# Between two edge passes of a graph network: another order for the first five tiles, and ScalarE's order written out

## The chip, the cores and the metric

The kernel runs on one core of a Trainium2 chip. The metric is device time in microseconds (us), the median of several executions. A core has five engines that run beside each other, each through its own queue in order: PE (TensorE, matrix products and transposes), DVE (VectorE), ACT (ScalarE), POOL (GpSimd, here the issuer of gathers) and SP (SyncE, here the issuer of DMA transfers).

## The reference

Two layers of a graph network on 3125 nodes with 256 features and 103125 edges. Each layer adds a graph part and an attention-like part to x, and then a mixture of experts. Cut to what lies around the change:

```python
xn = _layernorm(x)
x = x + edge_max(xn, src, dst) + mix0(xn)            # first edge pass
z = _layernorm(x)
x = x + layer_norm(moe(z) + z) * gamma + beta        # two experts for all tokens
xn = _layernorm(x)
# second edge pass: relational graph convolution
W = einsum("rb,bio->rio", comp, basis)               # 8 relations
h_all = einsum("ni,rio->nro", xn, W)                 # a table of 3125 x 8 rows
agg = segment_sum(h_all[src, edge_type], dst)
x = x + layer_norm(gelu(agg + xn @ loop_w + h_bias + xn)) + attention(xn)
x = x + moe(layer_norm(x))                           # top 2 of 8 experts for each token
```

Layer 0's router works on the mean over all nodes, so both experts and their weights are the same for all tokens, but known for certain only once every node has gone through the first pass.

## The kernel before, in words

The nodes lie in 25 tiles of 128 (the last is short). In the first pass POOL gathers rows of neighbours, DVE takes the maximum, and a queue of background jobs works off what follows. The experts are guessed from the means of the first tiles and their products run in the background of the pass. At its end tile 0 alone is left: `settle` fixes the router's weights (`w_first`, the first expert's weight, L1491) and whether the guess failed (`missed`, L1489); PE has meanwhile computed tile 0's hidden products into two PSUM banks (`phs`, `hidden_products`, L1515). All engines then read `missed` (L1953) and branch (L1954); the body of that branch, which repeats the experts' work with other weights, is not entered in these runs.

The stretch after the branch makes the second pass's table, tile by tile from tile 24 down to tile 0. A class `Four` takes the tiles in groups of `cuts`: two (24, 23), three (22 to 20), four, four, four, four, three and one. A group's vector work has four steps, each a list of one job for each tile:

- `mixed` (L2008): z is the sum of both experts' outputs, with statistics; after the last tile ScalarE takes a square root (L2016).
- `added` (L2020): subtract the mean, scale.
- `summed`: reciprocal (L2025), add to x (L2026), statistics; after the last tile a second root (L2032).
- `normed`: reciprocal (L2037), normalize (L171); z is then ready for its table.

`table(j, between)` makes the table of one tile: `to_xT` transposes z on PE (L182) and copies it on ScalarE (L183); four blocks of products follow (L188, 512 columns each; `mm`, four PSUM banks), each evacuated into `hs` by ScalarE (blocks 0 and 2, L177) or DVE (blocks 1 and 3, L175; for tile 24 all four on DVE, L2057); then SP stores 1 MB to `htab` (L2061). After each block the jobs of `between[b]` are issued: the steps of the next group, and after them sums of early gathers (L2114). How they are spread is this line, for the list `mine` of a table's jobs:

```python
per = -(-len(mine) // 4)
four.table(j, [mine[per * b : per * (b + 1)] for b in range(4)])
```

`early` lets POOL fetch own rows and, from about the tenth table on, edge rows of four tiles whose tables are ready. Which, and when, is fixed when the program is built.

Inside `tc.manual_schedule(engines=...)` the named engines run in the program's order; the other engines' order is chosen by the framework's planner. Before, DVE and POOL are named, so ScalarE and PE are planned: ScalarE may copy the transposed z of two tiles ahead of evacuations and roots. Tile 0's gelus (`hidden_gelus`, L1524), output products (`outputs_a`: two bias matmuls L1529, sixteen matmuls L1532) and their copies (`outputs_out`, L1542 and L1543) come in the program ahead of the first table; `outputs_b` follows five tables later.

In this text tables and joins are counted from 0: table 0 is tile 24's, table 24 is tile 0's, and join 5-6 is the place between tables 5 and 6. After the tables the second pass gathers with POOL, and its background jobs hold attention and the experts.

Of the kernel before, what the change touches and what calls it, by code (L numbers as in the profile page):

```python
# [11 lines left out]
F32 = mybir.dt.float32  # L12
BF16 = mybir.dt.bfloat16
I32 = mybir.dt.int32
AF = mybir.ActivationFunctionType
# [5 lines left out]
P = 128  # L21
# [33 lines left out]
GROUPS = tuple(range(a, b) for a, b in zip(CUTS, CUTS[1:])) + (range(0, 1),)  # L55
# [45 lines left out]
def gps_kernel(ctx: ExitStack, tc: tile.TileContext, a, out):  # L101
    nc = tc.nc
    V, S, G, PE = nc.vector, nc.scalar, nc.gpsimd, nc.tensor
# [45 lines left out]
    def bcast_load(name, ap, n, pool):  # L149
        t = pool.tile([P, n], F32, name=name)  # L150
        S.dma_start(t, bass.AP(tensor=ap.tensor, offset=ap.offset, ap=[[0, P], [1, n]]))
        return t
# [801 lines left out]
    with ExitStack() as prx:  # L954
        prx.enter_context(
            tc.manual_schedule(
                engines={mybir.EngineType.DVE, mybir.EngineType.Pool, mybir.EngineType.PE, mybir.EngineType.SP}
# [328 lines left out]
        steps = pre.tile([P, NT], F32, name="steps")  # L1286
# [31 lines left out]
    def fast():  # L1318
# [76 lines left out]
        mv2 = keep.tile([P, NT, 2], F32, name="mv")  # L1395
        rs2 = keep.tile([P, NT], F32, name="rs")
        f0k = f0h = f0b = None
        w1 = w2 = b1 = b2 = w_rel = basis = gam = bet = w_first = missed = guessed = part = inside = None
        pmean = [None]

        def begin():
            nonlocal f0k, f0h, f0b, w1, w2, b1, b2, w_rel, basis, gam, bet, w_first, missed, guessed, part, inside
            f0k = f0x.enter_context(tc.tile_pool(name="f0k", bufs=1, side="right"))
            f0h = f0x.enter_context(tc.tile_pool(name="f0h", bufs=2, side="right"))
            f0b = f0bx.enter_context(tc.tile_pool(name="f0b", bufs=1, side="right"))
            w1 = f0k.tile([P, 2, 2, F], F32, name="w1_0")
            w2 = f0k.tile([P, 2, FC, D], F32, name="w2_0")
            b1 = f0k.tile([P, 2, FC], F32, name="b1_0")
            b2 = f0k.tile([1, 2, D], F32, name="b2_0")
            w_rel = f0k.tile([P, 2, NX * D], F32, name="w_rel")  # L1410
            w_first = f0k.tile([P, 1], F32, name="w_first")
            missed = f0k.tile([1, 1], I32, name="missed")
            guessed = f0k.tile([P, 2, NX], F32, name="guessed")
            part = f0k.tile([P, 2], F32, name="part")
            basis = f0b.tile([P, 4, 2, D], F32, name="basis")
            for b in range(4):
                nc.sync.dma_start(basis[:, b, :, :], a["basis"][b].rearrange("(c p) o -> p c o", p=P))
            gam = bcast_load("gam0", a["f0_gamma"], D, f0k)
            bet = bcast_load("bet0", a["f0_beta"], D, f0k)
            inside = f0k.tile([P, 1], F32, name="inside")  # L1420
            V.tensor_scalar(inside, pcol, LAST - 0.5, None, op0=ALU.is_lt)
# [56 lines left out]
        def settle():  # L1478

            mean = f0k.tile([P, 2], F32, name="mean_b")  # L1480
            V.tensor_tensor(mean, part, pmean[0], op=ALU.add)
            V.tensor_scalar(mean, mean, 1.0 / NN, None, op0=ALU.mult)
            w_full, rank = settled[:] = yield from route(mean, "b")
            tmp = f0k.tile([P, NX], F32, name="tmp_b")
            hit = f0k.tile([P, 2], F32, name="hit")
            V.tensor_tensor(tmp, guessed[:, 0, :], guessed[:, 1, :], op=ALU.add)
            V.scalar_tensor_tensor(tmp, rank[:, 0, :], 1.5, tmp, op0=ALU.is_lt, op1=ALU.mult)
            V.reduce_sum(hit[:, 0:1], tmp, axis=AX.X)
            V.tensor_scalar(missed, hit[0:1, 0:1], 1.5, None, op0=ALU.is_lt)  # L1489
            V.tensor_tensor(tmp, w_full[:, 0, :], guessed[:, 0, :], op=ALU.mult)  # L1490
            V.reduce_sum(w_first, tmp, axis=AX.X)  # L1491
# [17 lines left out]
        def hidden_products(ts, i, ph=None):  # L1509

            at0 = ts[0] * P
            ph = ps_mm.tile([P, 512], F32, name="mm") if ph is None else ph
            for f in range(FC):
                for c in range(2):
                    PE.matmul(  # L1515
                        ph[:, f * P : (f + 1) * P], w1[:, i, c, f * P : (f + 1) * P], xT[:, c, at0 : at0 + P],
                        start=(c == 0), stop=(c == 1),
                    )
            return ph

        def hidden_gelus(ts, i, ph):
            hT = hTs[i] = f0h.tile([P, FC, 3 * P], F32, name=f"hT0_{i}", bufs=1)
            for f in range(FC):
                S.activation(hT[:, f, :P], ph[:, f * P : (f + 1) * P], AF.Gelu, bias=b1[:, i, f : f + 1])  # L1524

        def outputs_a(ts):
            for j, t in enumerate(ts):
                py = pys[t] = ps_mm.tile([P, 512], F32, name="mm")
                PE.matmul(py, ones_row, b2.rearrange("o i d -> o (i d)"), start=True, stop=True)  # L1529
                for i in range(2):  # L1530
                    for f in range(FC):
                        PE.matmul(  # L1532
                            py[:, i * D : (i + 1) * D], hTs[i][:, f, j * P : (j + 1) * P], w2[:, i, f, :],
                            start=False, stop=(f == FC - 1), skip_group_check=True,
                        )

        def outputs_out(ts):

            for t in ts:
                py = pys.pop(t)  # L1540
                y1 = seconds[t] = f0h.tile([P, D], F32, name="y1", bufs=SECONDS)
                S.copy(xT[:, :, t * P : (t + 1) * P], py[:, :D].rearrange("p (c n) -> p c n", c=2))  # L1542
                S.copy(y1, py[:, D:])  # L1543

        def outputs_b(ts):


            for t in ts:
                y1 = seconds.pop(t)
                d = xT[:, :, t * P : (t + 1) * P]  # L1550
                V.tensor_tensor(xt_tok[:, t, :], xt_tok[:, t, :], y1, op=ALU.add)
                V.tensor_tensor(d, d, y1.rearrange("p (c n) -> p c n", c=2), op=ALU.subtract)
# [12 lines left out]
        with ExitStack() as l0x:  # L1565
# [376 lines left out]
            ET = mybir.EngineType  # L1942
            with tc.manual_schedule(engines={ET.DVE, ET.Pool, ET.PE, ET.Activation}):
                fin[0].sums(0)
                fin[0].norms()
                routing = settle()
                next(routing)
                ts = GROUPS[-1]
                phs = [hidden_products(ts, i) for i in range(2)]
                for _ in routing:  # L1950
                    pass

        again = nc.values_load(missed[0:1, 0:1])  # L1953
        with tc.If(again > 0):  # L1954
# [33 lines left out]
        sump = fx.enter_context(tc.tile_pool(name="sump", bufs=1))  # L1988
        sums = sump.tile([P, len(EARLY), D], F32, name="sums")
        with ExitStack() as tx:  # L1990
            tx.enter_context(tc.manual_schedule(engines={mybir.EngineType.DVE, mybir.EngineType.Pool}))
            tp = tx.enter_context(tc.tile_pool(name="tp", bufs=2, side="right"))
            ready = []

# [130 lines left out]
            fours = [Four(range(a, b)) for a, b in cuts]  # L2125

            first, second = fours[0].steps(), fours[1].steps()
            for part_ in (first[0], second[0], first[1], second[1], first[2], first[3], second[2]):
                for job in part_:
                    job()  # L2130
            for i in range(2):
                hidden_gelus(GROUPS[-1], i, phs[i])
            outputs_a(GROUPS[-1])
            outputs_out(GROUPS[-1])
            for four, after in zip(fours, fours[1:] + [None]):
                steps = after.steps() if after is not None else []
                if four is fours[0]:
                    steps = second[3:]
                each = -(-len(steps) // four.k)
                if four is fours[2]:  # L2140
                    outputs_b(GROUPS[-1])
                for j in range(four.k):
                    mine = [job for part_ in steps[each * j : each * (j + 1)] for job in part_]
                    while adds and adds[0][0] + 4.0 < TABLE * len(ready):
                        mine.append(lambda a=adds.popleft(): add_up(*a[1:]))
                    per = -(-len(mine) // 4)
                    four.table(j, [mine[per * b : per * (b + 1)] for b in range(4)])
                    ready.append(four.tiles[j])
                    early(len(ready) - 1)
# [9 lines left out]
        with ExitStack() as l1x:  # L2159
# [18 lines left out]
            b1 = l1w.tile([P, NX, FC], F32, name="b1")  # L2178
# [401 lines left out]
    with tc.If(unfit < 1):  # L2580
        fast()
# [78 lines left out]
```

## Time and profile before

| | |
|---|---|
| median of 6 runs | 2987.46 us (2967.22 to 2996.63) |
| the profiled execution | 2989.64 us |
| its span | 2987.9 us |
| granted TensorE clock, mean | 0.762 |
| busy: PE, PE weight loads, DVE, ACT, POOL | 63%, 40%, 42%, 19%, 58% |
| end of the first pass's routing (w_first) | 1428.2 us |
| first table product | 1445.16 us |
| last store of the table issued | 1643.2 us |
| second pass's own gathers begin | 1660.49 us |

In a line of the profile's timeline stand the start (us from the span's start), the length, the engine, the line of the kernel, the operation, what it writes and reads with its size, and in square brackets how long the engine was idle before it and what ended that. Lines named PE are matmuls, PEld weight loads; a `q` behind an engine's name is its instruction queue.

### The profile page before, as it was taken

The page shows a single profiled execution, that of the slowest core. Times are in us where ns is not written, and L with a number is a line of the kernel's source. Part 1 is how long each engine was busy: PE and PEld are TensorE (multiplying, and loading weights), DVE is VectorE, ACT ScalarE, POOL GpSimd, SP SyncE. Part 2 cuts the span into 40 slices and gives each one's busy share as a digit, 9 for nine tenths or more (in the row PEclk, how much of TensorE's full clock was granted, in tenths as well). Part 3 has the DMA queues.
Part 4 walks back from the last instruction along what each step waited for, and adds up shares of the span by engine and source line. Part 5 has one row for each costly group of instructions (what it writes and reads, how often), then busy time and mean ns, then how long its engine had stood idle before and what let it go on. Part 6 is the DMA issues. An engine that isn't in the chain of part 4 may idle for free.

```text
span 2987.9 us, 20996 instructions
## 1 busy us (share of the span) xinstructions
PE 1881.3 (63%) x6033; PEld 1182.6 (40%) x6033; DVE 1256.7 (42%) x3537; ACT 558.5 (19%) x1275; POOL 1724.5 (58%) x1830
## 2 busy tenths in 40 slices
PE   4374657403473653366898348867786786866877
PEld 2232324202341422244443124554454454654656
DVE  7443434526324433344664333334343334343342
ACT  5122221000110101011321112122111121222233
POOL 5566566676647566655036755565666566656561
PEclk9675777655785776677899667887898888877978
DMA  5533333333323233322256632232232222222220
GB/s 178 137 86 91 82 87 101 93 107 110 93 62 105 67 96 85 94 67 77 97 197 223 197 111 67 80 89 80 84 92 86 78 82 82 86 77 84 76 80 18
DMA packets 125962, 290.09 MB, mean 97 GB/s; under 512 B 41386, under 2 KB 63982, under 8 KB 122632
## 3 DMA queue, kind: packets, MB, share of 16 engines
q0 software_dynamic: 83184, 230.02, 27.1%
q1 hardware_dynamic: 38122, 55.88, 5.5%
q10 hardware_dynamic: 4526, 2.71, 0.4%
q8 instruction: 51, 0.84, 0.1%
q14 instruction: 79, 0.65, 0.1%
HBM read 249.07 MB, written 39.41 MB: 97 GB/s over the span
## 4 chain that ended last, share of the span: by engine, by line
PE 21%; issue 10%; another core or an unknown queue 9%; DVE 5%; POOL 4%; ACT 2%; DMA 1%; DVEq 0%; POOLq 0%; ACTq 0%
PE mm L2408 8%; PE py L2439 6%; PE mm L188 4%; POOL gt L193 4%; DVE gt L1356 1%; DMA gt<-htab_f,idx2g 1%; DVE bnst L162 1%; PE pctx L2247 1%; PE pt L2378 1%; PE mm L2302 1%; DVE x L2458 1%; ACT hT L2412 0%; PE mm L2300 0%; DVE acc L1361 0%
## 5 line engine op out<-in xcount | busy, mean ns | idle before, releaser
L193 POOL DMA_INDIRECT gt<-btab,idx x814 | 799.8, 983 | 485.4 <-issue 228.3
L193 POOL DMA_INDIRECT gt<-htab_f,idx2g x742 | 732.4, 987 | 487.0 <-DVE acc L1361 244.6
L2439 PE MATMUL py<-w,hT 128*128 128x256 f32 (+1 forms) x1600 | 403.0, 402 | 113.0 <-issue 70.0
L2408 PE MATMUL mm<-xT,w 128*128 128x256 f32 (+4 forms) x1408 | 419.7, 452 | 85.8 <-issue 50.4
L1356 DVE TENSOR_TENSOR gt<-gt 128x256 f32<-128x256 f32 (+1 forms) x767 | 410.0, 535 | 113.0 <-remote 58.6
L2439 PEld LDWEIGHTS py<-w,hT 128*128 128x128 f32 (+1 forms) x1600 | 314.4, 200 | 187.6 <-issue 107.5
L2408 PEld LDWEIGHTS mm<-xT,w 128*128 128x128 f32 x1408 | 266.7, 216 | 220.2 <-issue 145.7
L2458 DVE SCALAR_TENSOR_TENSOR x<-py,wf,x 128x256 f32<-128x256 f32 x200 | 87.9, 478 | 513.5 <-remote 248.6
L2412 ACT ACTIVATE hT<-mm,b 128x256 f32<-128x256 f32 (+4 forms) x352 | 168.1, 496 | 600.0 <-remote 251.6
L188 PE MATMUL mm<-w_rel,xT 128*128 128x512 f32 x400 | 180.2, 609 | 10.0 <-ACT xT L183 9.4
L1503 PE MATMUL mm<-xT,w 128*128 128x384 f32 (+2 forms) x320 | 118.2, 537 | 104.6 <-issue 61.3
L1532 PE MATMUL mm<-w,hT 128*128 128x256 f32 x400 | 132.6, 491 | 64.3 <-issue 40.5
L1361 DVE TENSOR_TENSOR acc<-acc,gt 128x256 f32<-128x256 f32 x371 | 158.3, 427 | 31.2 <-DVE gt L1356 13.5
L1532 PEld LDWEIGHTS mm<-w,hT 128*128 128x128 f32 x400 | 94.7, 247 | 117.9 <-issue 72.1
L1503 PEld LDWEIGHTS mm<-xT,w 128*128 128x128 f32 x320 | 72.5, 253 | 148.8 <-issue 88.9
L188 PE MATMUL mm<-w_qkv,xT 128*128 128x512 f32 (+1 forms) x200 | 104.2, 646 | 32.4 <-ACT vs L1751 32.0
L1863 PE MATMUL pmean<-ones,xt 128*128 128x1 f32 (+1 forms) x100 | 21.2, 316 | 159.4 <-DVE xt L171 159.4
L188 PEld LDWEIGHTS mm<-w_rel,xT 128*128 128x128 f32 x400 | 76.8, 195 | 105.7 <-issue 88.9
L188 PE MATMUL pt<-w_own,xT 128*128 128x256 f32 x100 | 42.1, 550 | 115.5 <-DVE acc L1845 52.8
L193 POOL DMA_INDIRECT gt<-htab_f,soon x72 | 73.7, 1024 | 46.2 <-issue 19.8
L1863 PEld LDWEIGHTS pmean<-ones,xt 128*128 128x128 f32 (+1 forms) x100 | 21.8, 301 | 169.3 <-DVE xt L171 167.7
L1507 ACT ACTIVATE hT<-mm,b 128x384 f32<-128x384 f32 (+2 forms) x80 | 40.3, 517 | 231.4 <-remote 149.2
(436 smaller groups left out, 2118.6 us busy)
## 6 DMA issues: line engine op xcount, KB each, us to landing
htab_f<-hs SPq DMA_DIRECT2D x25, 1024.0 KB
gt<-btab,idx POOLq DMA_INDIRECT x814
gt<-htab_f,idx2g POOLq DMA_INDIRECT x742
w<-in_f_W_dram SPq DMA_DIRECT2D x20, 512.0 KB
ntab<-x SPq DMA_DIRECT2D x5, 640.0 KB
btab<-bs SPq DMA_DIRECT2D x5, 640.0 KB
x<-in_x_dram SPq DMA_DIRECT2D x4, 640.0 KB
otab<-xn SPq DMA_DIRECT2D x16, 128.0 KB
```

Source lines behind the costliest of these rows:

```text
L188: PE.matmul(ps, lhs[:, c, t * P : (t + 1) * P], w[:, c, :], start=start and c == 0, stop=stop and c == 1)
L193: G.indirect_dma_start(out=dst, out_offset=None, in_=table, in_offset=bass.IndirectOffsetOnAxis(ap=idx, axis=0))
L1356: V.tensor_tensor(gt[:, :h, :], gt[:, :h, :], gt[:, m - h : m, :], op=op)
L1361: V.tensor_tensor(acc, own(t) if i == 0 else acc, gt[:, 0, :], op=op)
L1503: PE.matmul(ph[:, :n], w1[:, i, c, f * P : (f + 1) * P], xT[:, c, at0 : at0 + n], start=(c == 0), stop=(c == 1),)
L1507: S.activation(hT[:, f, :n], ph[:, :n], AF.Gelu, bias=b1[:, i, f : f + 1])
L1532: PE.matmul(py[:, i * D : (i + 1) * D], hTs[i][:, f, j * P : (j + 1) * P], w2[:, i, f, :], start=False, stop=(f == FC - 1), skip_group_che ...
L1863: PE.matmul(pmean[0][:, c : c + 1], xt_tok[:r, t, c * P : (c + 1) * P], ones[:r, 0:1], start=(t in (1, SEEN + 1) and c == 0), stop=(t in ( ...
L2408: PE.matmul(ph[:, :n], w1s[e][:, c, f * P : (f + 1) * P], xT[:, c, at0 : at0 + n], start=(c == 0), stop=(c == 1),)
L2412: S.activation(hT[:, f, :n], ph[:, :n], AF.Gelu, bias=b1[:, e, f : f + 1])
L2439: PE.matmul(py[:r, j * D : (j + 1) * D], hT[:, f, at : at + r], w2s[e][:, f, :], start=(f == 0), stop=(f == FC - 1),)
L2458: V.scalar_tensor_tensor(d, y, wf[:r, t, e : e + 1], d, op0=ALU.mult, op1=ALU.add)
```

## The change

The first two tiles go through all four steps ahead of everything else, with one `mixed` job of the next group between their last two steps. The rest of that group's steps, tile 0's gelus, its output products and their copies become jobs among tables 0 and 1. ScalarE joins DVE and POOL in the program's order for the whole stretch. A square root of `w_first` into a tile that nothing reads is added at the end of the routing. The number of all other operations stays.

```diff
@@ begin()
+            w_first_root = f0k.tile([P, 1], F32, name="w_first_root")
@@ end of the routing, ahead of the branch
                 for _ in routing:
                     pass
+                S.activation(w_first_root, w_first, AF.Sqrt)
@@ the stretch of the tables
-            tx.enter_context(tc.manual_schedule(engines={mybir.EngineType.DVE, mybir.EngineType.Pool}))
+            tx.enter_context(tc.manual_schedule(engines={ET.DVE, ET.Pool, ET.Activation}))
...
             first, second = fours[0].steps(), fours[1].steps()
-            for part_ in (first[0], second[0], first[1], second[1], first[2], first[3], second[2]):
-                for job in part_:
-                    job()
-            for i in range(2):
-                hidden_gelus(GROUPS[-1], i, phs[i])
-            outputs_a(GROUPS[-1])
-            outputs_out(GROUPS[-1])
+            ahead_ = second[0].pop(0)
+            for job in first[0] + first[1] + first[2] + [ahead_] + first[3]:
+                job()
             for four, after in zip(fours, fours[1:] + [None]):
                 steps = after.steps() if after is not None else []
                 if four is fours[0]:
-                    steps = second[3:]
+                    ts = GROUPS[-1]
+                    gelus = [lambda i=i: hidden_gelus(ts, i, phs[i]) for i in range(2)]
+                    outs = [lambda: outputs_a(ts), lambda: outputs_out(ts)]
+                    steps = [gelus + second[0], second[1], second[2] + outs, second[3]]
                 each = -(-len(steps) // four.k)
```

Spread over tables 0 and 1, the jobs fall so: table 0 has both gelu jobs after block 0, two `mixed` after block 1, `added` after blocks 2 and 3; table 1 has two `summed` after block 0, one `summed` and `outputs_a` after block 1, `outputs_out` and one `normed` after block 2, two `normed` after block 3.

More of the change, by code (lines that the diff above doesn't have):

```diff
@@ L1397, in fast @@
         f0k = f0h = f0b = None
-        w1 = w2 = b1 = b2 = w_rel = basis = gam = bet = w_first = missed = guessed = part = inside = None
+        w1 = w2 = b1 = b2 = w_rel = basis = gam = bet = w_first = missed = guessed = part = inside = w_first_root = None
         pmean = [None]
         def begin():
-            nonlocal f0k, f0h, f0b, w1, w2, b1, b2, w_rel, basis, gam, bet, w_first, missed, guessed, part, inside
+            nonlocal f0k, f0h, f0b, w1, w2, b1, b2, w_rel, basis, gam, bet, w_first, missed, guessed, part, inside, w_first_root
             f0k = f0x.enter_context(tc.tile_pool(name="f0k", bufs=1, side="right"))
```

## The prediction

> **What bounds the kernel now.** The page first: no engine is full over the span (PE 63%, POOL 58%), so the place decides. The change touches only the stretch between the two edge passes; by busy time per stretch it has two parts, 1428.0 to 1445.2 us, where PE works at a granted clock of 0.63, and 1445.2 to 1643.2, the 25 tables, where PE is busy 185.43 of 198.00 us at 0.96. Then ScalarE's timeline and the timeline of all engines over the first part:
>
> ```profile
> 1432.46 1.28 ACT L1524 ACT_TABLE_LOAD   x1 [5.99 <-PEq L1954]
> 1433.76 1.14 ACT L1524 ACTIVATE hT<-mm,b 128x128 f32<-128x128 f32 x4
> 1434.91 1.28 ACT L2016 ACT_TABLE_LOAD   x1
> ...
> 1439.62 1.28 ACT L1524 ACT_TABLE_LOAD   x1
> 1440.91 0.88 ACT L1524 ACTIVATE hT<-mm,b 128x128 f32<-128x128 f32 x3
> 1441.81 1.28 ACT L2032 ACT_TABLE_LOAD   x1
> 1443.11 0.21 ACT L2032 ACTIVATE rs<-rs 128x2 f32<-128x2 f32 x1
> ```
>
> ScalarE swaps function tables six times between gelus and roots. It starts only when PE is through the branch of L1954. The root that the first two tiles need, ready to be taken at 1440.36, comes at 1443.11. What waits:
>
> ```profile
> 1440.19 0.17 DVE L2031 TENSOR_SCALAR rs<-mv 128x2 f32<-128x2 f32 x1
> ...
> 1443.34 0.17 DVE L2037 RECIPROCAL rs<-rs 128x2 f32<-128x2 f32 x1 [2.99 <-ACT rs L2032]
> ...
> 1443.55 0.74 DVE L171 TENSOR_SCALAR z<-x,mv,rs 128x256 f32<-128x256 f32 x2
> ...
> 1445.16 7.15 PE L188 MATMUL mm<-w_rel,xT 128*128 128x512 f32 x11
> ```
>
> So the first table product starts at 1445.16. From there PE sets the pace: a table is 16 matmuls of 0.429 us, 6.86 us. The timeline later in this stage shows how two tables join:
>
> ```profile
> 1491.22 0.60 PE L182 MATMUL pt<-ident,z 128*128 128x128 f32 x4
> 1491.42 0.69 DVE L175 COPY hs<-mm 128x512 f32<-128x512 f32 x1 [0.62 <-PE mm L188]
> 1491.63 0.65 ACT L183 COPY xT<-pt 128x256 f32<-128x256 f32 x2 [1.35 <-PE pt L182]
> 1492.03 0.47 DVE L2008 SCALAR_TENSOR_TENSOR z<-xT,w_first,xt 128x256 f32<-128x256 f32 x1
> 1492.06 14.00 PE L188 MATMUL mm<-w_rel,xT 128*128 128x512 f32 x32 [0.24 <-ACT xT L183]
> ...
> 1493.21 0.17 DVE L2015 TENSOR_SCALAR rsz<-mvz 128x4 f32<-128x4 f32 x1
> ...
> 1493.42 0.20 ACT L2016 ACTIVATE rsz<-rsz 128x4 f32<-128x4 f32 x1 [1.14 <-DVE rsz L2015]
> ```
>
> Two tiles are transposed together and ScalarE copies both, so 32 matmuls run without a break; a break costs about 0.95 us, once per pair. The root comes after both copies. The last view is the chain that ended last: over 1445 to 1582 it is these matmuls, then gathers on POOL, which from 1626.95 on stops for nothing and reaches the second pass's own gathers at 1660.49. A delay of the tables up to about 1590 therefore reaches the end one for one; I take all of it, and half as the lower bound, as POOL waited only 4.4 us in all between 1558 and 1605.
>
> **The change part by part.** The profiled execution took 2989.64 us (span 2987.9), 2.2 above the median of 2987.46; I work out a difference and add it to the median.
>
> *The first two tiles go ahead.* DVE leaves the branch at 1430.08 as now. By today's rows: two `mixed` and the sum end at 1432.49, where ScalarE, idle after its own branch at 1429.1, takes the root (0.20). Two `added` (0.41 each) cover that. Two `summed` at 1.08 reach 1435.6, the sum and root 1436.1, one `mixed` of the next tiles (1.1) covers the root until 1437.0, reciprocal 0.2, normalize 0.41: z at 1437.7. Today it is 1443.55 + 0.41 = 1443.96. **-6.3 us** for the first table product, now at 1438.9. PE's branch ended at 1432.3 and hinders nothing.
>
> *The extra root before the branch* runs in ScalarE's wait between 1426.5 and 1428.2: table load 1.28, root 0.20 after w_first. It delays ScalarE's read of `missed` by up to 0.4, which ends before 1432.5: zero. If the table were loaded again after the branch, 1429.1 to 1432.5 hides 1.28 too; uncovered it would cost 1.3.
>
> *The gelus and products go into the tables.* Eight gelus and two table loads lie on ScalarE beside table 0, whose evacuations are all on DVE: hidden by 9 us of PE work. The products are new on PE's busy path: today they lie in its idle time (1432.70 to 1443). In the first pass the same rows took 1.12 (two bias matmuls, L1529) and 3.72 (sixteen, L1532), 4.8; scaled to the 0.429 of a 512-column matmul 0.86 + 3.4 = 4.3. I take **+4.5**. The two hidden-product banks stay held until the gelus are done, about 3.6 us into table 0, when the third product block needs one: just covered. The copies of `outputs_out` and `outputs_b` come 25 us before their reader. No DMA moves; SP's and POOL's program orders stay.
>
> *The other three tiles* run on DVE beside tables 0 and 1. The join 0-1, free today, waits for their root: +0.9. Joins 1-2 to 3-4: -0.2 in all (today 0.8, 0, 1.75; then 0.8, 1.0, about 0.6, as the third evacuation waits behind a root). Up to table 4: -6.3 + 4.5 + 0.9 - 0.2 = **-1.1**.
>
> *ScalarE in order* is the added wait. The xT copy of the next tile is in the program behind everything of this table, its root too. For four tiles and no gather sums, `per` is 1: the last `mixed` or `summed`, with the root, stands behind the fourth block's evacuation. So after tables 5, 7, 9 and 11 PE waits for DVE's evacuation, one job, the root, and only then the copy. From the rows: evacuation starts 1491.42, 0.2 after PE's end; root done 1493.62; copy 0.37; matmul 0.05 to 0.24 later: 1494.2, a gap of 3.0 where today one sees 0.86. Behind the root on ScalarE stand that copy and all evacuations of the next table; PE waits for both. While PE waits it can transpose the tile after, as today, which frees one later join unless z is not ready (8-9 and 12-13: normalized only inside tables 8 and 12). Joins 5-6 to 14-15 today: 0.86 + 5 x 0.96 = 5.7. After: 4 x 3.0 + 2 x 0.95 + 1.4 (13-14: here the root stands before the third evacuation, copy chain 1550.9 to 1552.0 against PE's end at 1550.6) = 15.3. **+9.6.** Joins 15-16 to 18-19, roots again before the third evacuation: **+1.0**. After that POOL carries the chain.
>
> Sum: -1.1 + 9.6 + 1.0 = +9.5; less a little, as POOL had waits to spare: **+9**.
>
> Two unknowns. Whether PE's transposes are still drawn ahead is the planner's choice; if never, all joins up to 19 cost 0.95 or more: +15 in place of +9 (I count 6 further joins). Bounds 0 and +6; I take 0, since today's rows show the pairing wherever PE waits for a copy. And the clock: after 1.75 us of PE idle (1475.7) matmuls came back at 0.43, after 7.26 (1610.72) at 0.85 for seven of them, 7 x 0.42 = 3.0 us. A gap of 3.0 lies between; four such gaps cost 0 to 12. I take 0, nearer to the 1.75.
>
> [...]
>
> **The rivals.**
> *B, slower.* The pairing is lost: +15. Or the four gaps also halve the clock: +9 + 12 = +21. One place, the copy behind the root; decisive once PE's transposes are not issued before the wait, or the gap passes what the clock bears. For: ScalarE can no longer copy two tiles at once, as the 0.65 us row does. Against: transposes lie on PE, whose order is still planned. 3002 to 3008.
> *C, about equal.* ScalarE's root does not hold PE: the planner puts other PE work into the gaps (the 16 products, transposes). Then only -1.1 stays, or -5 with every pair join freed: 2983 to 2986. Against: nothing of PE's is ready there but one transpose pair.
> *D, faster.* Not by the parts named: -6.3 and six freed joins of 0.95 less 4.5 is -7.5 at most. It would need a different planned order in the second pass, or the loss of the stall at 1603 to 1610.7; that one shows late evacuations on all engines and belongs to no part of the change.
> *The change does nothing*: the order is fixed by the program on DVE and ScalarE, so the first z must move; I give this no chance.
>
> **How the numbers follow.** A, +9: 2987.5 + 9 = 2996.5, chance 0.46, own range 2988 to 3004. B 0.34; C 0.12; D 0.08. A measurement of this kernel can tell about 0.5%, 14.9 us, from no change: the bounds are 2972.5 and 3002.4. B's 0.34 and 0.08 of A lie above, 0.42; D and a little of C lie below, 0.10; the rest 0.48. The range goes from 2978 (C, less the 10 us that single runs scatter) to 3016 (B with clock, less its rarest end).
>
> **What would show it.** In the changed profile: no table load between 1432 and 1438, first `hs` matmul near 1439; sixteen L1532 matmuls between table products; after tables 5, 7, 9 and 11 an xT copy that directly follows a root and a PE gap near 3 us; the first second-pass gather near 1669 in place of 1660.5. Wrong if the xT copies keep ahead of the roots, if table 5 starts at 1484 but table 15 no later than 1560, or if the second pass takes another length than 1327.4 us by more than the table stage moves.

## The result, and the profile after

The changed kernel takes 2992.32 us (median of 36 runs, 2959.72 to 3015.47), the kernel before, run beside it, 2978.66 us (78 runs): a ratio of 1.0042, 95% interval 1.0025 to 1.0058. The difference of the medians is +13.7 us; the forecast was +9 and 2996.5 us. The interval lies above 1, so the changed kernel is slower, by less than the 0.5% that the prediction took as the least that can be told. Ratios leave out runs more than 1.5% above the fastest of their kernel and medians don't, so that the two can differ by some tenths of a per cent. The profiled execution of the changed kernel took 2997.97 us, its span 2996.2, granted clock 0.759.

Single runs of one kernel differ by some 50 us, four times the effect. The traces show where much of that scatter lies: in the nine that took between 2974 and 3007 us the first pass ends (`w_first` written) anywhere from 1405 to 1441 us, and the second pass, from its first own gather to the end, takes 1320.0 to 1335.9 us; these last two are the same kernel (e1 and e11 below). So all readings below count from `w_first`, as the change adds nothing ahead of it but the table load of one root, and the stretches are compared one by one:

| us | before | after |
|---|---|---|
| span's start to `w_first` | 1428.02 | 1425.58 |
| `w_first` to the first table product | 17.14 | 10.68 |
| first table product to table 19 | 142.80 | 164.18 |
| table 19 to the second pass's first own gather | 72.53 | 69.44 |
| that gather to the end | 1327.4 | 1326.3 |

The first of the touched stretches got shorter by 6.46 us, the tables longer by 21.4; 3.1 us are given back behind them, and the rest differs by far less than it scatters. From `w_first` to the gathers it is +11.8 us.

**The start.** ScalarE's timeline after the change, from the branch on:

```profile
1427.59 1.28 ACT L2018 ACT_TABLE_LOAD   x1 [1.60 <-DVEq L1956]
1430.09 0.20 ACT L2018 ACTIVATE rsz<-rsz 128x2 f32<-128x2 f32 x1 [1.22 <-DVE rsz L2017]
1433.40 0.21 ACT L2034 ACTIVATE rs<-rs 128x2 f32<-128x2 f32 x1 [3.11 <-DVE rs L2033]
1435.83 0.37 ACT L183 COPY xT<-pt 128x256 f32<-128x256 f32 x1 [2.23 <-PE pt L182]
1436.22 1.28 ACT L1525 ACT_TABLE_LOAD   x1
1437.52 2.18 ACT L1525 ACTIVATE hT<-mm,b 128x128 f32<-128x128 f32 x8
1439.71 1.28 ACT L2018 ACT_TABLE_LOAD   x1
```

Line numbers of the changed kernel are one higher than before ahead of the branch and two higher behind it. The first two tiles' roots no longer stand behind gelus: the one that the first two tiles need comes at 1433.40, 7.8 us after `w_first`, where it came 15.1 after. The gelus and their two loads follow behind the first copy. The load at 1427.59 is there although a load of 1.28 us, at 1424.05, stands ahead of the extra root too, which is also a square root.

PE's timeline in tables 0 and 1 shows the moved products:

```profile
1436.26 9.04 PE L188 MATMUL mm<-w_rel,xT 128*128 128x512 f32 x16
...
1449.16 1.12 PE L1530 MATMUL mm<-b,ones 1*128 1x512 f32 x2
1450.21 3.72 PE L1533 MATMUL mm<-w,hT 128*128 128x256 f32 x16
1453.77 3.60 PE L188 MATMUL mm<-w_rel,xT 128*128 128x512 f32 x8
```

They take the place of table products from 1449.16 to 1453.77, 4.6 us.

**The joins.** The timeline of PE, DVE and ScalarE between tables 5 and 6:

```profile
1487.68 0.60 PE L182 MATMUL pt<-ident,z 128*128 128x128 f32 x4
...
1487.88 0.69 DVE L175 COPY hs<-mm 128x512 f32<-128x512 f32 x1 [0.62 <-PE mm L188]
...
1489.68 0.17 DVE L2017 TENSOR_SCALAR rsz<-mvz 128x4 f32<-128x4 f32 x1
...
1489.88 0.21 ACT L2018 ACTIVATE rsz<-rsz 128x4 f32<-128x4 f32 x1 [3.13 <-DVE rsz L2017]
1489.99 0.35 ACT L183 COPY xT<-pt 128x256 f32<-128x256 f32 x1
```

PE's transposes are done at 1488.28. ScalarE has nothing to do then and waits 3.13 us in all for the operand of its root, while the copy that PE waits for stands behind that root: evacuation, one `mixed` job, root, copy. The same on PE alone, with all four such places:

```profile
1490.40 15.70 PE L188 MATMUL mm<-w_rel,xT 128*128 128x512 f32 x32 [2.12 <-ACT xT L183]
...
1508.65 8.68 PE L188 MATMUL mm<-w_rel,xT 128*128 128x512 f32 x16 [2.34 <-ACT xT L183]
...
1518.01 7.13 PE L188 MATMUL mm<-w_rel,xT 128*128 128x512 f32 x16 [0.24 <-ACT xT L183]
...
1527.71 15.70 PE L188 MATMUL mm<-w_rel,xT 128*128 128x512 f32 x32 [2.34 <-ACT xT L183]
...
1546.02 8.77 PE L188 MATMUL mm<-w_rel,xT 128*128 128x512 f32 x16 [2.39 <-ACT xT L183]
```

The gaps are there, and behind each the group itself is longer: 32 matmuls take 15.70 us where they took 14.00, 16 take 8.68 and 8.77 where they take 7.13. The busy time per stretch gives the reason (length, busy us of PE, PEld, DVE, ACT and POOL with their instructions, granted clock, DMA share, GB/s), ahead of a gap, right behind it, and later:

```profile
1481.00:1487.60 6.60, 6.60 (x16) 2.80 (x16) 5.04 (x13) 1.17 (x2) 0.98 (x1) 1.00 0.52 199
1490.40:1494.80 4.40, 4.40 (x7) 1.86 (x8) 0.00 (x0) 0.59 (x1) 0.95 (x1) 0.61 0.45 177
1495.20:1504.40 9.20, 9.20 (x23) 4.17 (x22) 5.38 (x14) 1.45 (x3) 0.00 (x0) 1.00 0.44 141
```

For 4.4 us behind the gap the granted clock is 0.61; behind the other three it is 0.55, 0.66 and 0.53 over 3.5 to 3.6 us. The four groups lose 1.70, 1.55, 1.70 and 1.64, together 6.6 us.

**The way to the end.** POOL's waits between 1560 and 1660 us, before and then after (what it waited for: us in total, times, longest):

```profile
POOL gt L193 <- DMA htab_f<-hs: 3.6, 2, 1.9
```

```profile
POOL gt L193 <- DMA htab_f<-hs: 12.3, 3, 6.9
```

The gathers wait 8.7 us longer for stored tables: the delay of the tables reaches the queue that sets the end.

### The profile page after: what moved, and what is told of

It reads as the page before. It is cut to its first block, busy times and chain, and to the rows that moved or that the text cites. A ratio compares the mean times of both kernels' runs of the same rounds, so it can differ in the third digit from the quotient of the medians.

```text
span 2996.2 us, 20993 instructions
## 1 busy us (share of the span) xinstructions
PE 1908.5 (64%) x6033; PEld 1185.4 (40%) x6033; DVE 1254.3 (42%) x3537; ACT 555.3 (19%) x1274; POOL 1722.8 (58%) x1830
## 5 line engine op out<-in xcount | busy, mean ns | idle before, releaser
L2409 PE MATMUL mm<-xT,w 128*128 128x256 f32 (+4 forms) x1408 | 431.0, 458 | 105.2 <-issue 60.8
L2440 PE MATMUL py<-w,hT 128*128 128x256 f32 (+1 forms) x1600 | 413.3, 410 | 86.5 <-issue 57.5
L2440 PEld LDWEIGHTS py<-w,hT 128*128 128x128 f32 (+1 forms) x1600 | 322.0, 204 | 165.8 <-issue 92.7
L188 PE MATMUL mm<-w_rel,xT 128*128 128x512 f32 x400 | 187.3, 626 | 14.5 <-ACT xT L183 13.9
L1533 PE MATMUL mm<-w,hT 128*128 128x256 f32 x400 | 122.4, 463 | 61.5 <-issue 52.0
L1533 PEld LDWEIGHTS mm<-w,hT 128*128 128x128 f32 x400 | 88.6, 231 | 107.0 <-issue 82.5
L188 PEld LDWEIGHTS pt<-w_own,xT 128*128 128x128 f32 x100 | 26.1, 284 | 130.4 <-issue 59.7
```

Source lines behind the costliest of these rows:

```text
L188: PE.matmul(ps, lhs[:, c, t * P : (t + 1) * P], w[:, c, :], start=start and c == 0, stop=stop and c == 1)
L1533: PE.matmul(py[:, i * D : (i + 1) * D], hTs[i][:, f, j * P : (j + 1) * P], w2[:, i, f, :], start=False, stop=(f == FC - 1), skip_group_che ...
L2409: PE.matmul(ph[:, :n], w1s[e][:, c, f * P : (f + 1) * P], xT[:, c, at0 : at0 + n], start=(c == 0), stop=(c == 1),)
L2440: PE.matmul(py[:r, j * D : (j + 1) * D], hT[:, f, at : at + r], w2s[e][:, f, :], start=(f == 0), stop=(f == FC - 1),)
```

## The experiments

The experiments ran on three chips. On two of them the kernel before takes 2986.81 us (35 runs) and 2987.57 (29 runs), on the third 2475.82 (17 runs). Each ratio is against the kernel before on the same chip, and that of the first two rows is the result above; the stretch from `w_first` to the second pass's first own gather, and the start of table 19, come from each kernel's profile. The kernel before has one profile, of about 2990 us; none was taken on the third chip.

| us after `w_first` | chip | table 0 | table 19 | own gathers | median of runs, ratio |
|---|---|---|---|---|---|
| before | – | 17.14 | 159.94 | 232.5 | |
| the change | – | 10.68 | 174.86 | 244.3 | 1.0042 [1.0025, 1.0058] |
| e1_act_free | 1st | 14.38 | 160.46 | 233.0 | 2989.87, 1.0008 [0.9970, 1.0046] |
| e3_copy_first | 1st | 10.68 | 160.21 | 230.0 | 2985.51, 1.0000 [0.9964, 1.0037] |
| e4_per2 | 1st | 10.67 | 161.05 | 228.1 | 2981.54, 0.9987 [0.9956, 1.0018] |
| e5_warm | 1st | 10.68 | 168.40 | 240.3 | 2991.47, 1.0022 [0.9990, 1.0054] |
| e9_change | 2nd | 10.66 | 175.05 | 245.9 | 2998.99, 1.0010 [0.9978, 1.0042] |
| e10_ahead_act_free | 2nd | 13.95 | 161.75 | 230.1 | 2988.33, 0.9996 [0.9964, 1.0027] |
| e11_act_free | 2nd | 14.18 | 160.59 | 231.7 | 2992.46, 1.0011 [0.9979, 1.0043] |
| e2_act_order_only | 3rd | 26.90 | 182.22 | 250.5 | 2497.44, 1.0084 [1.0068, 1.0099] |
| e6_no_root | 3rd | 10.68 | 175.14 | 242.1 | 2493.09, one run |
| e8_warm_one | 3rd | 10.67 | 168.77 | 236.9 | 2489.14, one run |
| e7_products_ahead | 3rd | 12.88 | 155.90 | 220.2 | 2472.20, 0.9983 [0.9973, 0.9993] |

**Is it ScalarE's order?** The theory: ScalarE's fixed order costs the tables some 16 us, 9.5 in gaps and 6.6 in the slow clock behind them. Undone alone:

```diff
-            tx.enter_context(tc.manual_schedule(engines={ET.DVE, ET.Pool, ET.Activation}))
+            tx.enter_context(tc.manual_schedule(engines={ET.DVE, ET.Pool}))
```

> The changed kernel with one part undone: ScalarE's order in the table stretch is the planner's again; the new order of the first five tiles stays. Theory (the loss is the copy that stands behind a root on ScalarE): the joins go back to about 0.95 us per pair, no PE gap near 3 us, no matmuls at 0.85 us after table 1; table 15 starts about 1 us ahead of where it did before the change (counted from DVE's leaving the branch, 128.5 us), and the time is 0 to 4 us below the kernel before (ratio 0.9985 to 1.0000). Rival (the loss is the products and steps that were moved among the tables): most of the 12 us stays, ratio 1.003 to 1.005.

PE's timeline of this kernel, in the place of the four gaps:

```profile
1483.48 14.00 PE L188 MATMUL mm<-w_rel,xT 128*128 128x512 f32 x32 [0.25 <-ACT xT L183]
1497.32 0.60 PE L182 MATMUL pt<-ident,z 128*128 128x128 f32 x4
1498.17 14.00 PE L188 MATMUL mm<-w_rel,xT 128*128 128x512 f32 x32 [0.24 <-ACT xT L183]
```

The pairs are back without a gap, every group of 32 from table 3 to table 20 takes 14.00, and table 19 starts 14.4 us earlier than with the change; from table 4 to table 19 it is 16.0 us, as the theory had it. The planner used its freedom at the start too: DVE waits 3.21 us for the first root and 0.30 for the second, where with the change it waits for neither, so that table 0 comes 3.7 us later (at 14.38), and those 3.7 are a part of the gain of 6.46 that is lost again. The time is level with the kernel before, not 0 to 4 us below it. The same kernel was later run beside the change itself (e9 and e11, below).

The part alone, on the kernel before:

```diff
-            tx.enter_context(tc.manual_schedule(engines={mybir.EngineType.DVE, mybir.EngineType.Pool}))
+            tx.enter_context(tc.manual_schedule(engines={ET.DVE, ET.Pool, ET.Activation}))
```

> The kernel before with one part of the change alone: ScalarE in the program's order in the table stretch; the old order of the first five tiles. Theory: the joins behind tables 5, 7, 9 and 11 open to about 3 us, with half-clock matmuls behind them (+15 in all), and the gelus, now behind all four roots, hold tile 24's copy, so that the first table product comes about 11 us later than before: table 19 near 184 us after the branch, ratio 1.0070 to 1.0100. Rival (only the joins count, the start gains as much as it loses): ratio 1.004 to 1.006.

ScalarE's timeline of this kernel, first rows behind the branch:

```profile
1208.40 0.20 ACT L2032 ACTIVATE rs<-rs 128x3 f32<-128x3 f32 x1 [4.59 <-DVE rs L2031]
1208.62 1.28 ACT L1524 ACT_TABLE_LOAD   x1
1209.92 2.17 ACT L1524 ACTIVATE hT<-mm,b 128x128 f32<-128x128 f32 x8
```

Written out, the old program puts the gelus behind all four roots and the first copy behind the gelus' products: table 0 starts 26.90 after `w_first`, 9.8 later than before. The four gaps come back (2.12, 2.34, 2.34, 2.38 us idle), three of them with a slow group behind (8.69, 15.70 and 8.79 us). The ratio, 1.0084, is clear of 1: this part makes the kernel slower, by 21.6 us of medians here. The start's 9.8 is a cost that the change itself does not have, because it also moves the gelus.

**Is it the place of the copy?** The order stays fixed, but the transposes and the copy of the next tile are issued after the fourth evacuation, ahead of that block's jobs and so ahead of the root:

```diff
+                def turned(self, j):
+                    to_xT(self.tiles[j], self.z[:, j, :])
-                def table(self, j, between):
-                    to_xT(t, self.z[:, j, :])
+                def table(self, j, between, after):
...
+                        if b == 3 and after is not None:
+                            after[0].turned(after[1])
```

> The changed kernel, but the transposes and the copy of the next tile are issued in the program after a table's fourth evacuation and ahead of the jobs behind it, so no root that stands after the fourth block is ahead of the copy; ScalarE stays in the program's order. Theory: the four gaps after tables 5, 7, 9 and 11 and the slow matmuls behind them go; what is left is joins behind a root that stands after the second block (13-14, 15-16), +1 to +2; the time is within 3 us of the kernel before (ratio 0.9990 to 1.0010). Rival (order on ScalarE as such, or the moved products): ratio 1.003 to 1.005.

ScalarE and PE around the join 5-6 of this kernel:

```profile
1503.52 0.60 PE L182 MATMUL pt<-ident,z 128*128 128x128 f32 x4
...
1503.93 0.37 ACT L183 COPY xT<-pt 128x256 f32<-128x256 f32 x1 [1.35 <-PE pt L182]
...
1504.36 14.00 PE L188 MATMUL mm<-w_rel,xT 128*128 128x512 f32 x32 [0.24 <-ACT xT L183]
...
1505.72 0.20 ACT L2018 ACTIVATE rsz<-rsz 128x4 f32<-128x4 f32 x1 [1.41 <-DVE rsz L2017]
```

The copy stands ahead of the root, the idle time is 0.24, and the whole 14.7 us at table 19 are gone. So it is not ScalarE's order as such but this one place in it. A second way to the same place, two jobs a block instead of one, so that no root stands behind the fourth evacuation:

```diff
-                    per = -(-len(mine) // 4)
+                    per = max(2, -(-len(mine) // 4))
```

> The changed kernel with one number changed: at least two jobs after each block, so that the root of a group of four stands after the second block and not after the fourth; PE's order of instructions is unchanged. Theory: the four gaps shrink from near 3 us to 1 to 1.5 us, and the clock stays whole, so of the 12 us about 10 go: ratio 1.0000 to 1.0020. Rival (the moved products, or a halved clock for another reason): no change of the ratio, 1.003 to 1.005.

PE's timeline of this kernel behind join 5-6:

```profile
1500.43 14.00 PE L188 MATMUL mm<-w_rel,xT 128*128 128x512 f32 x32 [0.24 <-ACT xT L183]
```

Table 19 starts at 161.05 in place of 174.86, 13.8 us earlier, by a change of one number that leaves PE's order as it is. The gathers start 4.4 us earlier than before although table 19 starts 1.1 us later; this one execution lacks a stall that the trace of before has (last section). By time it can't be told from the kernel before.

**Is the slow clock a cost of its own?** The gaps are kept, and PE is given something to do in them: two calls that multiply into a bank that nothing reads, ahead of the next tile's transposes.

```diff
+                        if b == 3 and len(ready) in (5, 7, 9, 11):
+                            warm = ps_acc.tile([P, 512], F32, name="warm", tag="acc1")
+                            for c in range(2):
+                                PE.matmul(warm, xT[:, c, t * P : (t + 1) * P], w_rel[:, c, :512], start=True, stop=True)
```

> The changed kernel with two more matmul calls of 512 columns, whose result nothing reads, behind the fourth block of tables 5, 7, 9 and 11: they lie in the four gaps. Theory (each gap costs its own length and 1.6 us more of half-clock matmuls behind it): gaps stay near 3 us from product to product, but the first matmuls behind them come at 0.43 us, not 0.85; 6 us of 12 go: ratio 1.0015 to 1.0030. Rival (the slow matmuls have another cause than the idle PE): they stay, ratio 1.004 to 1.005.

The timeline of this kernel at join 5-6, and the stretch behind the gap:

```profile
1486.73 1.88 PE L2063 MATMUL warm<-w_rel,xT 128*128 128x512 f32 x4
...
1488.44 0.60 PE L182 MATMUL pt<-ident,z 128*128 128x128 f32 x4
...
1489.04 0.35 ACT L183 COPY xT<-pt 128x256 f32<-128x256 f32 x1
...
1489.45 11.00 PE L188 MATMUL mm<-w_rel,xT 128*128 128x512 f32 x25 [0.40 <-ACT xT L183]
```

```profile
1489.45:1493.85 4.40, 4.40 (x11) 2.01 (x12) 0.61 (x2) 0.59 (x1) 0.95 (x1) 1.00 0.45 175
```

The copy still stands behind the root, and the useful matmuls start as late as with the change; but in the same 4.4 us eleven matmuls begin where seven did, at a granted clock of 1.00. Table 19 starts 6.46 us earlier than with the change; 6.6 was expected from the lengths of the four groups. With about half as much work in the gaps no group behind them is slow either:

```diff
-                            for c in range(2):
+                            for c in range(1):
```

> As the kernel with two extra matmul calls in the four gaps, but with one: PE's idle stretch between the transposes and the first product is near 1.4 us, between the 1.2 us or less that kept the clock and the 2.1 us that halved it. Theory (a stretch below 2 us is borne): all matmuls behind the gaps come at 0.43 us. Rival (the clock falls with any wait over 1.3 us): some at 0.85 us.

```profile
1251.91 1.02 PE L2063 MATMUL warm<-w_rel,xT 128*128 128x512 f32 x2
...
1254.63 14.00 PE L188 MATMUL mm<-w_rel,xT 128*128 128x512 f32 x32 [1.26 <-ACT xT L183]
```

That is PE's timeline of e8 at the same join. With 1.26 to 1.52 us idle the groups behind the gaps take 14.00 and 7.13 us, and table 19 starts 6.4 us earlier than in e6, which has the change's gaps on the same chip.

**Does the extra root do anything?**

```diff
-                S.activation(w_first_root, w_first, AF.Sqrt)
```

> The changed kernel without the added square root of w_first. Theory (it does nothing: the table is loaded again after the branch, in ScalarE's wait): the same load stands after the branch, the first root comes at the same 2.45 us after DVE leaves the branch, and all later steps too. Rival: the first root comes 1.3 us later.

```profile
1188.39 1.28 ACT L2017 ACT_TABLE_LOAD   x1 [2.73 <-SPq L1955]
1191.71 0.20 ACT L2017 ACTIVATE rsz<-rsz 128x2 f32<-128x2 f32 x1 [2.04 <-DVE rsz L2016]
```

ScalarE's timeline without the extra root: the first root ends waiting for DVE's operand either way, the load before it is hidden in that wait, and the first `mixed` is 2.06 us after `w_first` with and without. Table 0 stays at 10.68, table 19 at 175.14. It is worth nothing.

**Can the start be had without the gaps, and without the products in the tables?** Tile 0's gelus ahead of the branch, in place of the extra root; its products ahead of the first table; two jobs a block as in e4:

```diff
-                S.activation(w_first_root, w_first, AF.Sqrt)
+                for i in range(2):
+                    hidden_gelus(ts, i, phs[i])
...
+            outputs_a(GROUPS[-1])
...
-                    steps = [gelus + second[0], second[1], second[2] + outs, second[3]]
+                    steps = [[lambda: outputs_out(GROUPS[-1])] + second[0], second[1], second[2], second[3]]
...
-                    per = -(-len(mine) // 4)
+                    per = max(2, -(-len(mine) // 4))
```

> A version that should beat both: the changed kernel with at least two jobs after each block (the roots no longer stand after the fourth), tile 0's gelus on ScalarE ahead of the branch in place of the extra root, and tile 0's sixteen products on PE ahead of the first table instead of inside table 1. Theory: PE works off the products at half clock in its wait, about 8 us from its end of the branch, so the first table product comes about 3 us later than in the changed kernel (near 11.7 us after DVE leaves the branch, against 8.6), but table 0 runs at full clock (about 7.1 us, not 9.0) and table 1 is 4.8 us shorter; table 19 starts about 156 us after the branch (157.9 before the change, 172.8 after): ratio 0.9980 to 1.0000. Rival (the products cost the same in either place, as they hold up the first transposes): table 19 at 159, ratio 0.9995 to 1.0015.

ScalarE's and PE's timeline of this kernel around the branch:

```profile
1188.28 2.18 ACT L1525 ACTIVATE hT<-mm,b 128x128 f32<-128x128 f32 x8
...
1192.70 2.04 PE L1530 MATMUL mm<-b,ones 1*128 1x512 f32 x2 [5.84 <-PEq L1958]
...
1194.67 5.61 PE L1533 MATMUL mm<-w,hT 128*128 128x256 f32 x16
```

The products fill PE's wait for z and end at 1200.3, where z's transposes begin. With the change the transposes begin 9.55 us after `w_first`, here 12.00, so the place in front is not free: table 0 starts 2.2 us later than there, but the 4.6 us among the tables are gone. The first tables then run as a whole pair of 14.00 us, and table 19 starts 4.0 us earlier than in the trace of before, which is from another chip.

The first `mixed` starts 4.63 us after `w_first` instead of 2.06. The gelus end at 1190.46 and do not explain that; DVE's timeline shows the wait:

```profile
1192.60 0.18 DVE L2074 TENSOR_SCALAR own_r<-idx2g 128x25 int32<-128x25 int32 x1 [4.03 <-PEq L1958]
```

This instruction ran well ahead of the branch with the change (at 1412.9). Here it is DVE's first behind the branch and waits until PE has left the branch. DVE's normalize starts at 1199.90 and PE's products end at 1200.3, so freeing DVE alone could not bring the transposes forward by much. Why the instruction lands there was not tried.

The ratio 0.9983 has its interval below 1: this version beats the kernel before, by 3.6 us of medians, on the chip where it ran. What each of its three edits is worth was not measured alone.

**On one chip, with longer series.** The change, the change without ScalarE's order, and e7 without ScalarE's order, 12 runs each:

> The change as it is, on one chip with the two kernels beside it, so that the parts are had by difference. From the profiles so far: start -6.3, products +4.5, queue of ScalarE about +16 (gaps 9.5, slow clock behind them 6.6), end of the tables +12 to +15 over the kernel before. Mine: ratio 1.004 to 1.006. Rival (the tables' delay is swallowed by POOL's waits later): 1.000 to 1.002.

> The change without its part on ScalarE's order, beside the change itself. The difference of the two is the price of that part: 14 to 15 us by the profiles (gaps and slow clock), so the change's ratio should stand 0.004 to 0.006 above this one's. This one against the kernel before: 0.9985 to 1.0005. Rival (the order matters only where the gathers wait late): difference under 0.002.

> Products and gelus of tile 0 ahead of the branch, as in e7_products_ahead, and ScalarE's order left to the planner, as in e1_act_free. With the pairs back, 25 tables have about 12 joins of 0.95 instead of joins at most 1.1 each: table 19 about 153 to 156 us after w_first, where e7 had 155.9 and the kernel before 159.9. Mine: ratio 0.997 to 0.999. Rival (the planned order costs what e1 showed, 1.0008, and the early products bring nothing to the end): 1.000 to 1.002.

By times this series decided little: the intervals are 0.6% wide and all three hold 1. The difference of 0.004 to 0.006 that was expected between e9 and e11 did not show: their ratios (1.0010 and 1.0011) differ by nothing, as the rival had it, although their medians differ by 6.5 us. With intervals that wide 0.004 is not excluded either. The expected 1.004 to 1.006 of e9 meets its interval only at the lower edge. The traces repeat to the tenth: e9 has the gaps of 2.12, 2.34, 2.34 and 2.38 us and table 19 at 175.05, e11 none of them and 160.59. By traces the price of ScalarE's order is 14.5 us at table 19 and 14.3 at the gathers, after the 3.5 us by which the planner's own order starts table 0 later. By times only e2 stands clear of 1, and 9.8 us of its loss lie in the start. On the third chip, where 17 runs of the kernel before lie between 2473.54 and 2484.09 us, the one run of e6, the change without its extra root, took 2493.09: a hint, from a single run, that the change costs time there too. e10, expected to reach table 19 at 153 to 156, brings table 17 to 139.97 after `w_first`, 5.3 us earlier than before, and then loses it in a stall of PE (last section):

```profile
1572.04 14.00 PE L188 MATMUL mm<-w_rel,xT 128*128 128x512 f32 x32 [0.24 <-ACT xT L183]
...
1593.82 16.04 PE L188 MATMUL mm<-w_rel,xT 128*128 128x512 f32 x32 [7.35 <-issue]
```

## Why the prediction was right, and where it was wrong

- **The start, -6.3: right.** Measured -6.46. The order by rows (the `mixed`, `added` and `summed` one after another, root under the next `mixed`) is what the trace shows.
- **The extra root, nothing: right**, with the case that was named: the load is made again behind the branch (1427.59) and is hidden: 1.22 us of waiting for DVE's operand lie behind it in the change and 2.04 in e6. The gelu at 1437.52 follows its 1.28 us load by 0.02.
- **The products, +4.5: right.** 4.6 measured. e7 shows an alternative that the prediction did not see: with the products in front of z table 0 starts 2.2 us later than with the change, and the 4.6 are gone.
- **Up to table 4, -1.1: right.** Counted from the first `mixed`, table 4 started 47.40 us in before and 46.30 after. Inside this sum two sizes were off and met: join 0-1 cost 0.4 in place of 0.9, joins 1-2 to 3-4 cost 0.3 more in place of 0.2 less.
- **The four gaps: the mechanism is right, the size a little high.** PE's idle time is 2.12 to 2.39, and from the end of one table's last matmul to the next's first it is 2.72 to 2.78 us instead of 3.0. From table 4 to table 15 it is +15.2, of which 6.6 are the clock: the joins cost +8.6, not +9.6. From table 15 to 19 it is +0.9 against +1.0. The pairing of transposes, whose loss was taken as 0, is there (four transposes together at 1487.68).
- **The clock, taken as 0 of 0 to 12: wrong, and this is the mis-sized term.** It is 6.6. The row it was taken from does not carry it: the 1.75 us between products at 1475.7 of the old trace held two pairs of transposes, and PE's idle time in it was 1.00. The other row of the sum, seven slow matmuls and 3.0 us, was too long for these gaps: four matmuls, 1.7 us. Taking a gap of 3.0 as free was the author's estimate from the first of these rows; here the matmuls came back slow after 2.34 to 2.39 us of idle PE every time, and after 2.12 three times out of four.
- **"Less a little" behind the tables: too little in this pair, open otherwise.** From table 19 to the gathers 3.1 us came back where 0.5 was allowed. The same kernel in e9 gave back 1.6, and single executions have stalls of several us in this stretch (last section).
- **Together.** +14.9 at table 19 against +9.5, +11.8 at the gathers against +9. The second pass had the same length in this pair, as said, but it scatters by 16 us for one kernel, so that this agreement is in part luck. The gathers began at 1669.88; "near 1669" was the forecast, but this execution also had a first pass shorter by 2.4 us. That the total came out near is luck in part: a missing 6.6 met 1.0 too much in the joins and 2.6 too little allowance behind the tables. Of rival B, the clock half happened, at half its price; its other half, lost pairs, did not. Rival C needed PE work in the gaps: e5 shows that such work hides the clock's part (6.46 us at table 19) and not the wait.

The forecast of 2996.5 us was 4.2 above the measured median, and this nearness is luck too: the 6 runs first shown had a median 8.8 us above that of the 78, and the difference was 4.7 us larger than forecast.

## What to carry to other kernels

When an engine that copies operands for TensorE is put into program order, look at what stands just ahead of each copy: one root that waits for another engine cost four gaps here, and moving the copy in front of it, or the job by one block, took all of them away. Price a gap on TensorE with the matmuls behind it: in the change 2.1 to 2.4 us of idle cost another 1.55 to 1.70. Where runs scatter more than the effect, measure from an event in the trace that the change does not touch; here that turned a scatter of tens of us into agreement within 0.2 us for the same code at table 19.

## What the runs showed of the hardware

The clock: behind tables 5, 7, 9 and 11 of the change, e9, e6 and e2, all twelve gaps with 2.34 to 2.39 us of idle PE were followed by a slow group (8.66 to 8.80 or 15.70 us). Of the four gaps with 2.12 us three were (the change, e9 and e6, 15.70), one was not (e2, 14.00). After 1.78 us (once, in the change at 1624) and after 1.26 to 1.52 us (e8, four gaps) the groups took their 7.13 or 14.00 us; behind the 1.78 the granted clock was 1.00 from 1624.04 to 1628. From product to product all sixteen gaps of those four kernels are about equally long, 2.72 to 2.78 us, and differ in whether two or four transposes lie in them; the runs do not tell whether transposes count as work for the clock. With products of 1.02 us in each gap (e8) no group behind them was slow.

The kernel before took 2986.81 and 2987.57 us on two chips and 2475.82 on a third. The traces show where the 17% lie: the tables take the same time there (table 19 at 175.14 in e6, at 174.86 in the change), but `w_first` comes at 1187 to 1191 us, and the second pass takes 1061 to 1065 us from its first own gather. Why was not tried.

One thing stays open. In the last six tables PE stops once or twice for 2 to 7 us: in the trace of before at 1603 (7.26), in the change, in e1, e3, e5, e9, e10 and e11, but not in e4, and in none of the four on the third chip. In e10 it takes more than the tables had gained. It moves the gathers of single traces by several us, so the 3.1 us that came back behind the tables, and e4's 4.4 us, can't be put down to the edits. No run was made for its cause.
